# Where the last quarter's sum is made: in SBUF by GpSimd, or in HBM by a DMA that adds

## The chip, the core and the metric

The kernel runs on one core of one Trainium2 chip. The metric is the device time of that core in microseconds (us). The engines are TensorE (PE: matmuls; PEld: its weight loads), VectorE (DVE), ScalarE (ACT), GpSimd (POOL) and SyncE (SP). SP issues most DMA transfers, on a queue of its own; POOL can issue some too, on another. All data and sums are 32-bit floats.

## The reference

The input x has 4096 rows (32 x 128 tokens) of 2048 features. A weight is quantized to levels of a codebook with a low-rank correction, x is multiplied by it, and the result goes through a linear layer with a routed low-rank mixture; x is added at the end:

```python
def _L0_cond_ref(x, weight, scale_log, codebook, lora_A, lora_B):
    lora_delta = lora_B @ lora_A * (LORA_ALPHA / LORA_RANK)
    ...
    idx = jnp.searchsorted(thresholds, normalized, side='left')
    quantized = cb[idx]
    ...
    w_eff = w_q + lora_delta
    return x @ w_eff.T

def _L0_ffn_ref(x, W_base, b_base, A_w, B_w, router_w, cores):
    result = jnp.einsum('bsd,od->bso', x, W_base) + b_base
    ax = jnp.einsum('bsd,rd->bsr', x, A_w)
    probs = jax.nn.softmax(jnp.einsum('bsd,ed->bse', x, router_w), axis=-1)
    per_expert = jnp.einsum('bsr,erq->bseq', ax, cores)
    mixed = jnp.einsum('bseq,bse->bsq', per_expert, probs)
    return result + jnp.einsum('bsr,or->bso', mixed, B_w) * SCALING

x = x + _L0_ffn_ref(_L0_cond_ref(x, ...), ...)
```

## The kernel before

The two large linear maps and the added x are first folded into one 2048 x 2048 matrix S (quantized weight times base weight, plus the identity). This first stage ends at about 1000 us of the profile. It writes S to HBM (`s_dram`) already in the form that the second stage wants: 49 combinations of its sixteenths, 1024 KB each.

The second stage computes the output, transposed, as S times x, by the Strassen-Winograd scheme on two levels: seven products instead of eight for 2 x 2 blocks, and each of the seven again by seven. The tokens are cut into 4 groups (`NG`) of 1024 (`TG`); each group takes 7 outer x 7 inner = 49 products (`NP`), so there are 196, numbered n. A product (`product`, L833) is 32 matmuls (L846) of a tile of S with a block of 256 columns of x or of a difference of such blocks (`t`, made by `inner`, L813). The outer products come in the order `OUTER = [1, 5, 6, 2, 3, 7, 4]`; within a group, outer product 1 is n = 0 to 6, 5 is 7 to 13, 6 is 14 to 20, 2 is 21 to 27, 3 is 28 to 34, 7 is 35 to 41, and 4 is 42 to 48.

Each group keeps four tiles of half the features by half the tokens in SBUF, 2 MB each, in pools with one buffer. They turn into the four quarters of the group's output:

- `M1` is outer product 1; with outer product 2 added it is the upper left quarter.
- `M5` is outer product 5.
- `U2` is outer product 6 plus M1. With outer product 7 added (n = 35 to 41) it is a sum, U3. From n = 45 on outer product 4 is subtracted from it in place, block by block, and it becomes the lower left quarter.
- `C12` is U2 + M5, taken at n = 22 before U2 gets outer product 7; with outer product 3 added it is the upper right quarter.
- The lower right quarter is U3 + M5. `join` (L957) makes it at n = 43 on GpSimd, in M5's place, as it makes C12 at n = 22: four sums of 128 x 1024 elements (L964).

A sum that writes a block of U2 after n = 43 must wait until whatever reads the old block is done: L912 (DVE) for the upper left block after n = 45; L937, L916 and L941 (POOL) after n = 46 for the lower ones.

The work around the products is written out by hand. `early`, `late` and `last` hold what is to be issued at each n of a group, and the loop at L1083 runs through all n: the `early` entries, the product, the `late` entries, the next `inner`, the load of S for product n + 3 (`load_s`, L797), and the sums that take product n - 1 out of PSUM (`after`, L918). Every engine and queue executes its own part of this in order. S has three buffers (`stp`), so the load for product n + 3 waits on SP until product n is done. At n = 43 `early` also loads four times 1024 KB of x for the next group (`load_x`, L790, `xA` and `xB`); at n = 15 two for xB. The stores are issued on SP too: `store_half` (L1029) stores half of a quarter's features, 1024 KB in rows of 2 KB.

PSUM is four tiles of two banks each (`ps_z`), taken in turn by the products.

Of the kernel before, what the change touches and what calls it, by code (L numbers as in the profile page):

```python
# [16 lines left out]
ALU = mybir.AluOpType  # L17
# [150 lines left out]
def adaln_ffn_kernel(  # L168
# [29 lines left out]
    nc = tc.nc  # L198
# [16 lines left out]
    HT = TG // 2  # L215
# [15 lines left out]
    NK = NS // 4  # L231
    HB = NK * 2
# [41 lines left out]
    with ExitStack() as sa:  # L274
# [371 lines left out]
        at = {}  # L646
# [63 lines left out]
        for i in range(4, NS):  # L710
            g, j = divmod(i, 4)
# [74 lines left out]
    outr = outT.rearrange("(c p) t -> p c t", p=P)  # L786
    state = {}
# [15 lines left out]
    def blk(x, a, b):  # L803
        return x[:, a * NK : (a + 1) * NK, b * QT : (b + 1) * QT]
# [83 lines left out]
    def new(t, g):  # L888
        state[t, g] = home[t].tile([P, HB, HT], F32, tag=t, name=f"{t}_{g}")
        return state[t, g]  # L890
# [63 lines left out]
                lambda d: nc.vector.tensor_tensor(d, state["u3", o], z["e"], ALU.subtract),  # L954
            )

    def join(t, g, parts):  # L957

        u = state["U2", g]
        m5 = state["M5", g]  # L960
        out = new("C12", g) if t == "C12" else m5
        for a in range(2):
            for b in range(2):
                nc.gpsimd.tensor_tensor(blk(out, a, b), blk(u, a, b), blk(m5, a, b), ALU.add)  # L964
# [64 lines left out]
    def store_half(t, g, ph, th, a):  # L1029
        c = HB * ph + NK * a  # L1030
        nc.sync.dma_start(outr[:, c : c + NK, ts(2 * g + th, HT)], state[t, g][:, ts(a, NK)])

    def store_last(t, g, ph, th):

        c = HB * ph + NK
        for h in range(2):
            to = outr[:, c + 2 * h : c + 2 * h + 2, (2 * g + th) * HT : (2 * g + th) * HT + QT]
            nc.sync.dma_start(to, blk(state[t, g], 1, 0)[:, 2 * h : 2 * h + 2])
# [3 lines left out]
    early, late, last = {}, {}, {}  # L1042

    def at(where, n, f, *args):
        where.setdefault(n, []).append((f, args))
# [12 lines left out]
    at(late, 12, softmax)  # L1058
    at(late, 15, flip)
    at(late, 17, mix)  # L1060
    at(late, 22, lambda g: join("C12", g, None))
    at(late, 43, lambda g: join("C22", g, None))
    for t, n, ph, th in (("M1", 29, 0, 0), ("C12", 36, 0, 1), ("M5", 44, 1, 1)):
        for a in range(2):
            at(late, n + 2 * a, lambda g, *a: store_half(a[0], g, *a[1:]), t, ph, th, a)
    at(late, 47, lambda g: store("U2", g, 1, 0, 0, 0))
    at(late, 49, lambda g: (store("U2", g, 1, 0, 0, 1), store("U2", g, 1, 0, 1, 1)))
    at(last, 49, lambda g: store_last("U2", g, 1, 0))


# [83 lines left out]
```

## Time and profile before

| | us |
|---|---|
| median of 3 runs (2416.7 to 2417.75) | 2417.7 |
| the profiled execution, its time | 2421.27 |
| its span, from the first to the last instruction | 2419.5 |
| mean granted TensorE clock | 0.990 |
| POOL: the four sums of `join` into C12, mean of one (L964, x16) | 2.841 |
| POOL: the four sums of `join` into M5, mean of one (L964, x16) | 2.349 |
| POOL: a DMA issue of 512 KB, mean (L585, x10) | 0.719 |

The span is cut by the profile into busy time by engine, groups of instructions by source line, waits, and the chain of work that ended last. A group line has the source line, engine, operation, output and inputs by name, their shape and the count; then busy time and mean duration, then idle time before it and what ended it. A timeline line has the start, the duration (of several merged instructions together with the gaps between them), engine, line, operation and count. A DMA line has the issuing queue, size, and the median time from issue to landing.

The page's account of the DMA queues (packets, MB, share of 16 engines over the span) and of HBM:

```profile
q1 hardware_dynamic: 143248, 547.39, 63.5%
q0 software_dynamic: 2560, 9.18, 1.0%
HBM read 455.07 MB, written 101.71 MB: 230 GB/s over the span
```

q1 is SP's queue. q0 is POOL's; before, only the last part of the first stage uses it.

### The profile page before, as it was taken

Reading aid. Unit: us, or ns where it says so; the run is one execution under the profiler, and the core shown is the slowest. Engines: PE = TensorE matmul, PEld = TensorE weight load, DVE = VectorE, ACT = ScalarE, POOL = GpSimd, SP = SyncE. Lnnn points to the kernel's source line nnn. Section 1 sums busy time; section 2 is a strip of 40 time slices with the busy share of each in tenths; the row PEclk is TensorE's granted clock in tenths of the full one; section 3 lists DMA queues with packets and bytes.
Section 4 is the critical chain, followed back from the end, with each engine's and each line's share of the span. In section 5 each row is a group of like instructions: output and inputs, shape, how many; then the busy total and the mean of one; then the engine's idle time right before and its main releaser. Section 6 shows DMA issues by size and latency. Waiting matters only on the chain.

```text
span 2419.5 us, 23942 instructions
## 1 busy us (share of the span) xinstructions
PE 2332.1 (96%) x10032; PEld 1633.4 (68%) x10032; DVE 925.1 (38%) x788; ACT 370.9 (15%) x411; POOL 1045.2 (43%) x520
## 2 busy tenths in 40 slices
PE   3779999999999999999999999999999999999999
PEld 2334444444444444688888888888888888888887
DVE  7633348446745730433321223222333222323321
ACT  3623332343234300000000000000000000000000
POOL 5747888667766731571413103313203114003133
PEclk9989999999999999999999999999999999999999
DMA  5569998756966695594366754466645557563654
GB/s 169 224 250 330 373 357 315 277 211 228 339 225 227 242 345 188 182 341 182 140 235 231 240 198 174 174 211 256 228 176 185 195 193 263 206 223 142 209 188 160
DMA packets 146393, 558.47 MB, mean 231 GB/s; under 512 B 14360, under 2 KB 24864, under 8 KB 105312
## 3 DMA queue, kind: packets, MB, share of 16 engines
q1 hardware_dynamic: 143248, 547.39, 63.5%
q0 software_dynamic: 2560, 9.18, 1.0%
q8 instruction: 79, 1.29, 0.2%
q10 hardware_dynamic: 464, 0.26, 0.0%
q14 instruction: 42, 0.34, 0.0%
HBM read 455.07 MB, written 101.71 MB: 230 GB/s over the span
## 4 chain that ended last, share of the span: by engine, by line
PE 89%; DMA 4%; POOL 1%; SPq 0%; ACT 0%; DVE 0%; issue 0%; DVEq 0%; POOLq 0%
PE z L846 56%; PE m L514 24%; PE m L490 4%; PE z L876 1%; PE acc L612 1%; DMA t_dram<-tt 1%; PE d L352 1%; DMA xs<-in_xT 1%; DMA tt<-in_wbT 1%; DMA wbp_raw<-in_wbT 1%; PE m_r L592 1%; PE mx_ps L1013 0%; POOL tt L641 0%; POOL tt L640 0%; POOL tt L639 0%; PE ra L970 0%
## 5 line engine op out<-in xcount | busy, mean ns | idle before, releaser
L846 PE MATMUL z<-t,s 128*128 128x256 f32 x3584 | 791.3, 380 | 0.0
L846 PEld LDWEIGHTS z<-t,s 128*128 128x128 f32 x3584 | 677.7, 190 | 102.8 <-issue 12.5
L370 DVE COPY_PREDICATED a<-above,step 128x1024 f32<-128x1024 uint8 x192 | 251.1, 1308 | 159.9 <-ACT above L369 144.1
L490 PE MATMUL m<-wbp_raw,a 128*128 128x512 f32 x512 | 239.5, 625 | 31.1 <-DVE a L395 29.3
L846 PE MATMUL z<-xA,s 128*128 128x256 f32 x1152 | 254.5, 379 | 0.0
L514 PE MATMUL m<-wbp_raw,a 128*128 128x512 f32 x576 | 253.1, 596 | 0.0
L514 PE MATMUL m<-wbp,a 128*128 128x512 f32 x576 | 251.6, 595 | 0.0
L937 POOL TENSOR_TENSOR c<-u,m 128x1024 f32<-128x1024 f32 x16 | 49.8, 3111 | 444.4 <-DVE u L934 423.0
L846 PEld LDWEIGHTS z<-xA,s 128*128 128x128 f32 x1152 | 218.9, 190 | 30.2 <-issue 0.5
L369 ACT ACTIVATE above<-w,neg_t 128x1024 fp8e5<-128x1024 f32 x192 | 205.3, 1139 | 130.9 <-POOL w L361 114.8
L490 PEld LDWEIGHTS m<-wbp_raw,a 128*128 128x128 f32 x512 | 100.2, 200 | 157.0 <-issue 122.9
L514 PEld LDWEIGHTS m<-wbp,a 128*128 128x128 f32 x576 | 108.1, 190 | 135.1 <-issue 130.3
L514 PEld LDWEIGHTS m<-wbp_raw,a 128*128 128x128 f32 x576 | 107.6, 190 | 135.7 <-issue 128.8
L846 PE MATMUL z<-xB,s 128*128 128x256 f32 x768 | 169.8, 379 | 0.0
L846 PE MATMUL z<-xC,s 128*128 128x256 f32 x768 | 169.7, 379 | 0.0
L846 PEld LDWEIGHTS z<-xB,s 128*128 128x128 f32 x768 | 145.8, 190 | 20.2 <-ACT m L932 0.4
L846 PEld LDWEIGHTS z<-xC,s 128*128 128x128 f32 x768 | 145.9, 190 | 19.8
L937 POOL TENSOR_TENSOR M<-u,m 128x1024 f32<-128x1024 f32 x8 | 24.8, 3104 | 303.5 <-DVE u L934 303.5
L926 ACT COPY m<-z 128x1024 f32<-128x1024 f32 x28 | 28.4, 1013 | 811.1 <-PE z L846 811.1
L389 POOL TENSOR_TENSOR a<-a,w 128x1024 f32<-128x1024 f32 x30 | 76.5, 2550 | 119.7 <-DVEq L380 99.4
L928 DVE TENSOR_TENSOR u<-z,m 128x1024 f32<-128x1024 f32 x28 | 34.2, 1223 | 217.8 <-issue 174.3
L395 DVE TENSOR_TENSOR a<-a,ds 128x1024 f32<-128x1024 f32 x32 | 85.2, 2662 | 81.6 <-POOL a L391 80.8
(216 smaller groups left out, 1997.2 us busy)
## 6 DMA issues: line engine op xcount, KB each, us to landing
s<-s_dram SPq DMA_DIRECT2D x196, 1024.0 KB, 4.9
wbp_raw<-in_wbT SPq DMA_DIRECT2D x76, 1024.0 KB, 6.7
wbp<-t_dram SPq DMA_DIRECT2D x48, 1024.0 KB, 6.3
xs<-in_xT SPq DMA_DIRECT2D x64, 512.0 KB, 8.1
xA<-in_xT SPq DMA_DIRECT2D x24, 1024.0 KB, 9.4
s_dram<-z SPq DMA_DIRECT2D x46, 512.0 KB, 4.6
w<-in_weight SPq DMA_DIRECT2D x32, 512.0 KB, 6.3
tt<-in_wbT SPq DMA_DIRECT2D x32, 512.0 KB, 9.0
```

What stands on the lines that cost most here:

```text
L352: nc.tensor.matmul(d[:, 4 * h + n, :], lora_BT_sb[rows, f, n, :], st[i]["la"][rows], start=True, stop=True)
L369: nc.scalar.activation(above, q, AF.Relu, bias=neg_t[:, r : r + 1], scale=GAIN, saturate=False)
L370: nc.vector.copy_predicated(a, above.bitcast(U8), step[:, r : r + 1].to_broadcast([P, F // 2]))
L389: v.tensor_tensor(a, a, w, ALU.subtract)
L395: nc.vector.tensor_tensor(a, a, st[i]["ds", f], ALU.add)
L490: nc.tensor.matmul(z, a[:, s, CM * c + m, :], t[:, m, :], start=f == 0 and c == 0 and m == 0, stop=f == 1 and c == 1 and m == CM - 1,)
L514: nc.tensor.matmul(z, a[:, s, CM * c + k, :], pieces[key][:, k, :], start=c == 0 and k == 0, stop=c == 1 and k == CM - 1,)
L592: nc.tensor.matmul(ps[RP * j : RP * j + RP, 0], ra_sb[:, m, :], a_half(i, m // HM)[:, m % HM, :], start=m < 4, stop=m >= NM - 4, tile_posi ...
L846: nc.tensor.matmul(z[:, c, :], s[:, k, ts(c, P)], rhs[:, k, :], start=not more and k == 0 and c % PER == 0, stop=k == NK - 1 and c % PER = ...
L926: nc.scalar.copy(temp("m1", o), z["a"])
L928: nc.vector.tensor_tensor(temp("u2", o), z["b"], state["m1", o], ALU.add)
L937: lambda d: nc.gpsimd.tensor_tensor(d, state["u3", o], state["m5", o], ALU.add),
```

## The change

The lower right quarter is no longer summed in SBUF. M5 is stored to its place in the output as soon as it is complete, at n = 16 and 18, and at n = 43 two DMAs issued by GpSimd add U2 (which then holds U3) onto it in HBM, half of the features each. `join` at n = 22 is unchanged.

```diff
-    def join(t, g, parts):
+    def join(g):
 
         u = state["U2", g]
         m5 = state["M5", g]
-        out = new("C12", g) if t == "C12" else m5
+        out = new("C12", g)
         for a in range(2):
             for b in range(2):
                 nc.gpsimd.tensor_tensor(blk(out, a, b), blk(u, a, b), blk(m5, a, b), ALU.add)
...
+    def store_more(t, g, ph, th, a):
+        c = HB * ph + NK * a
+        nc.gpsimd.dma_start(
+            outr[:, c : c + NK, ts(2 * g + th, HT)], state[t, g][:, ts(a, NK)], accum_op=ALU.add
+        )
+
...
-    at(late, 22, lambda g: join("C12", g, None))
-    at(late, 43, lambda g: join("C22", g, None))
-    for t, n, ph, th in (("M1", 29, 0, 0), ("C12", 36, 0, 1), ("M5", 44, 1, 1)):
+    at(late, 22, join)
+    for a in range(2):
+        at(late, 43, lambda g, a: store_more("U2", g, 1, 1, a), a)
+    for t, n, ph, th in (("M5", 16, 1, 1), ("M1", 29, 0, 0), ("C12", 36, 0, 1)):
         for a in range(2):
             at(late, n + 2 * a, lambda g, *a: store_half(a[0], g, *a[1:]), t, ph, th, a)
```

## The prediction

> **What bounds the kernel now.** I read the page first, then the chain of waits, then the time windows, the timeline and the DMA issues around the place that is changed. The page's busy row, its chain and two windows of the first group, at the place where GpSimd now sums (the columns of a window: stretch, its length, busy time of PE, PEld, DVE, ACT and POOL with counts, clock, DMA share, GB/s):
>
> ```profile
> PE 2332.1 (96%) x10032; PEld 1633.4 (68%) x10032; DVE 925.1 (38%) x788; ACT 370.9 (15%) x411; POOL 1045.2 (43%) x520
> PE 89%; DMA 4%; POOL 1%; SPq 0%; ACT 0%; DVE 0%; issue 0%; DVEq 0%; POOLq 0%
> 1311.60:1318.80 7.20, 7.20 (x35) 6.33 (x34) 0.67 (x1) 0.58 (x1) 6.51 (x3) 1.00 0.91 334
> 1318.80:1326.00 7.20, 7.20 (x35) 6.35 (x34) 0.56 (x1) 0.96 (x1) 0.00 (x0) 1.00 1.05 387
> ```
>
> TensorE sets the time. From 1001.7 us on it runs the 4 groups of 49 products with no gap worth the name: a group takes 353.15 us (the chain's pieces at 1348.01, 1701.15 and 2054.30), some 7.2 us a product. In the two windows PE is full and the clock is 1.00, while POOL works or idles as it likes. But the last two columns say that the DMA engines are also full here, at 334 to 387 GB/s. So at this place TensorE and the DMA engines have no room left, and GpSimd has plenty.
>
> The timeline of the same place (start, duration, engine, line), and issues with their time to landing; the last three lines are narrow stretches around one issue each, the S load for product 46 of groups 0, 1 and 2:
>
> ```profile
> 1305.62 3.26 POOL L916 TENSOR_TENSOR U<-U,c 128x1024 f32<-128x1024 f32 x1 [3.80 <-DVE c L954]
> 1308.84 9.27 POOL L964 TENSOR_TENSOR M<-U,M 128x1024 f32<-128x1024 f32 x4
> 1341.44 3.20 POOL L937 TENSOR_TENSOR c<-u,m 128x1024 f32<-128x1024 f32 x1 [23.33 <-DVE u L934]
> 1332.86 7.17 PE L846 MATMUL z<-t,s 128*128 128x256 f32 x32
> 1311.16 0.32 SPq L800 DMA_DIRECT2D s<-s_dram  x1
> 1311.53 0.98 SPq L794 DMA_DIRECT2D xA<-in_xT  x2
> 1312.55 2.93 SPq L794 DMA_DIRECT2D xB<-in_xT  x2
> 1318.07 0.34 SPq L800 DMA_DIRECT2D s<-s_dram  x1
> 1318.45 0.43 SPq L1031 DMA_DIRECT2D outT<-M  x1
> ...
> s<-s_dram SPq DMA_DIRECT2D x1, 1024.0 KB, 11.2
> s<-s_dram SPq DMA_DIRECT2D x1, 1024.0 KB, 13.2
> s<-s_dram SPq DMA_DIRECT2D x1, 1024.0 KB, 11.3
> ```
>
> SP issues S of product 45 at 1311.16, four loads of x for the next group (4 x 1024 KB), and at 1318.07 S of product 46, which sits behind them; product 46 begins at 1332.86. The load lands 11.2 us after its issue, at 1329.3: 3.6 us to spare. In group 1 it is issued at 1671.2, lands 13.2 us later at 1684.4, and is wanted at 1686.0 (353.14 us after group 0): 1.6 us. In group 2: 2024.35 + 11.3 = 2035.65, wanted at 2039.15: 3.5 us. Of all 196 S loads the median lands in 4.9 us; this one is the tight one. The first half of the M5 store, issued at 1318.45, stands behind it in the same queue.
>
> **The change, part by part.**
>
> *Removed: four GpSimd sums a group*, 9.27 us on the POOL row above. Worth nothing: after them POOL idles 23.33 us until L937. Without that cover they would delay L937, and by it the U2 stores. M5's buffer comes free earlier too, but its next writer is the next group's second outer product (n = 56 on), ten products after the last of its stores now.
>
> *Moved: the two M5 stores, from n = 44 and 46 to 16 and 18, on SP's queue.* They wait for nothing there: M5's last block is written at 1103.02 (DVE, L954), and SP comes to n = 16 at about 1113.8. At n = 15 SP loads 2 x 1024 KB of xB; the windows of group 0 there (7.2 us each) show a DMA share of 1.01 from 1109.8 to 1117.0 and 0.50 in the next. The store's first half adds 1.05 MB; at 0.395 MB/us (the saturated windows' 387 to 410 GB/s) that is 2.7 us, just what the half-empty window holds. It is issued behind the S load of product 18, so the next one (19) could be the late one; that has about 10 us of room (14.8 us from issue to use, 4.9 to land). The second half meets a window with share 0.12 or 0.45. Cost 0; if all of it collided, 2.7 us of those 10.
>
> *Added: two DMA issues on POOL at n = 43*, each 1024 KB. The trace has POOL issues of plain stores: 572 ns for 256 KB (L583), 720 ns for 512 KB (L585), so by a straight line 1.0 us for 1024 KB, and perhaps twice that if each row also needs its read described. POOL reaches the place at 1308.84, as the sum does now, so both are out by about 1311 to 1313. The price lies in the 23.33 us of idleness: 0. Their wait for the M5 stores, made at n = 18, has long been over at n = 43. Behind them on POOL stands nothing before L937.
>
> *Added: the transfers.* No row of this trace shows a DMA that adds. Call f its engine time as a multiple of a plain transfer of the same 1.05 MB. Low end: the row of the M5 store, which it resembles on the outside, f = 1. Above: it must fetch the destination from HBM as the xA load does (1024 KB, 9.4 us to land) and read SBUF and write HBM as the M5 store does (1024 KB, 11.9 us): one of each, f = 2. Far end: nothing overlaps, and each packet pays the round trip of the smallest load, 1.8 us (8 KB of cores). POOL's queue moves 9.18 MB in 2560 packets, 3.6 KB each, so a half has 18 per engine: 33 us, f = 33/2.66 = 12. I take f = 2, because the load and the store are the two rows that it is made of, and the S, x and POOL rows of this trace overlap their round trips well enough to reach 390 GB/s.
>
> Do they share engines with SP's loads? An S load issued at 1036.2 us beside 1.84 MB of POOL stores landed in 8.2 us instead of 4.8, in windows with a share of 1.02 to 1.04. So yes.
>
> Sum: up to the landing of S 46 the engines must now do 2.1 f MB more. Two credits: the stretch from 1309 to 1312 moves 0 GB/s now, and gives the POOL queue about 1.25 us alone (0.5 MB); and of the M5 store some 0.55 MB went through beside S 46 (6.84 MB moved from 1312 to 1330, of which S 45, x and S 46 are 6.29), which is gone. Delay = (2.1 f - 1.05) / 0.395: f = 1: 2.7 us; f = 2: 8.0; f = 3: 13.3; f = 4: 18.6. Less the room of 3.6, 1.6 and 3.5 us in groups 0, 1, 2: at f = 2 PE stops for 4.4 + 6.4 + 4.5 = 15.3 us; at f = 1, 1.1 us; at f = 3, 31.2; at f = 4, 47.1. Group 3 loads no further x (its windows show share 0.42 there), so 0. Nothing wins this back: PE is full before and after. S 47 is 2.7 us behind S 46 in the queue and wanted 7 us behind it: no second stall. DVE's L912 (1333.03, waits for the first half to be read) and POOL's L916 at 1344.71 (second half) come after the loads that are late, so they add nothing until f is near 4.
>
> The tail: PE ends at 2414.56, the span at 2419.5, with the same last U2 stores: 0. The sum against the profiled execution: span 2419.5 + 15.3 = 2434.8. That run took 2421.27, 3.6 above the median of 2417.7; on the median, 2433.0.
>
> The Trainium skill has a rule that speaks against the change. "Collectives: The Full Stack", on the bandwidth ceiling, says that an add in a DMA is slowed not by the arithmetic but by its two source reads, with a measured ratio of 62.28 to 32.35, or 1.93. No row here shows such a transfer; by that figure the stalls would be 4.0 + 6.0 + 4.1 = 14.1 us, beside 15.3 by the rows.
>
> **The rivals.** *No visible stall:* one pass, or SP's queue served ahead of POOL's. For it: 1 MB stores from SBUF do run beside loads at 390 GB/s. Against: the destination has to be read somewhere. It decides below f = 1.35, where the stalls sum to 4.8 us. At f = 1: 2417.7 + 1.1 = 2418.8. This is the case on the other side.
>
> *The transfers land too late:* f of 4 and more, up to 12, with the engines idle between round trips, so that SP's loads slip through but the transfers end late. At the far end the second half lands 66 us after issue, near 1375, and L916 at 1344.71 is 30 us late; SP's store of that block (n = 49, issued at 1355.56 now) holds SP until some 1377, with S loads behind it that have 10 us of room: 11 us a group, 33 in three. In the last group 2368.3 + 66 = 2434, then three POOL operations of 2.35 and a store of 7.7 us: 2449, 29 past the present end. In all 62: 2480. For it: each row waits for its own read. Against: the same is true of any copy.
>
> *Faster through a freer GpSimd or buffer:* nothing on PE's rows waits for the sums. The only part that PE does not fill is the 4.9 us of the tail; even half of it would be 2.4 us: 2415.3.
>
> **How the numbers follow.** 0.2% is 4.8 us, about what a measurement of this kernel can tell from no change. Forecast (f from 1.35 to 4; 2423 to 2465, 2433.0 the likeliest): 0.62. Late landing: 0.10. No visible stall: 0.25. Faster: 0.03. So slower 0.72, same 0.25, faster 0.03. The range goes from 2417, f = 1 with nothing lost, to 2466, f = 4.
>
> **What would show it.** Right: PE's weight load of product 46 waiting for S in groups 0 to 2 and not in 3, S 46 landing some 19 to 21 us after issue, POOL's queue larger by 8.4 MB (4 groups of 2.1) or twice that if both reads are counted, HBM reads up by 8.4 MB, gaps of 4 to 6 us. S 46 landing in less than 14 us would show that f is smaller than I take it, or that SP's queue is favoured. Wrong: gaps at another product, such as 19 (M5 stores) or 52 (SP held by a U2 store), or POOL's issues taking over 20 us.

## The result, and the profile after

The changed kernel takes 2444.3 us (median of 4 runs, 2442.9 to 2445.5) beside 2417.3 before (also 4 runs, one more than in the table above): 27.0 us slower, a ratio of 1.0112 (95% interval 1.0094 to 1.0129). The forecast was 2433.0, in a range of 2417 to 2466: the sign and the place are as forecast, the loss is 1.8 times the 15.3 us of the sum.

The page after (busy time; queue POOL: packets, MB, share; HBM; a group of PE):

```profile
PE 2334.9 (96%) x10032; PEld 1637.9 (67%) x10032; DVE 923.7 (38%) x788; ACT 370.8 (15%) x411; POOL 1018.5 (42%) x512
...
q0 software_dynamic: 6784, 17.57, 3.0%
...
HBM read 455.07 MB, written 110.10 MB: 231 GB/s over the span
...
L846 PE MATMUL z<-t,s 128*128 128x256 f32 x3584 | 798.5, 382 | 20.4 <-DMA s<-s_dram 20.4
```

The last line reads, before:

```profile
L846 PE MATMUL z<-t,s 128*128 128x256 f32 x3584 | 791.3, 380 | 0.0
```

POOL lost its sums, and with the new issues it is busy 27 us less in all; PE did not wait for any of that. PE's busy time has hardly changed, but a group of its matmuls that never stood idle now does, for 20.4 us, on the loads of S. The waits of PE in the second stage name the same 20.4 us in three places (total, times, longest):

```profile
PE z L846 <- DMA s<-s_dram: 20.4, 3, 7.0
```

Where it happens, in the timeline of the first group:

```profile
1304.57 2.64 POOL L1035 DMA_DIRECT2D outT<-U  x2
1306.90 0.32 SPq L800 DMA_DIRECT2D s<-s_dram  x1
1307.28 2.78 SPq L794 DMA_DIRECT2D xA<-in_xT  x2
1310.10 10.12 SPq L794 DMA_DIRECT2D xB<-in_xT  x2
1320.33 25.50 SPq L800 DMA_DIRECT2D s<-s_dram  x4
1327.52 1.15 PE L876 MATMUL z<-mx,bw_sb 17*128 17x256 f32 x16
1335.51 9.97 PE L846 MATMUL z<-t,s 128*128 128x256 f32 x32 [6.84 <-DMA s<-s_dram]
```

The adding transfers go out at 1304.57, the four x loads just behind them. Before, the second pair of x loads was issued within 2.93 us; now SP is held for 10.12 us while it issues them. So S of product 46, the first of the four in the line, is issued only at 1320.33 and lands 15.1 us later, at 1335.4:

```profile
s<-s_dram SPq DMA_DIRECT2D x1, 1024.0 KB, 15.1
```

Product 46 could have begun at about 1328.7 and begins at 1335.51. Groups 1 and 2 show the same (waits of 6.55 and 6.97 us), group 3, which loads no further x, nothing.

One more thing is in the last line of the timeline: the product that follows the wait takes 9.97 us, not 7.17. The windows around it show the clock (the last three columns are the granted clock, DMA share and GB/s):

```profile
1327.50:1328.70 1.20, 1.17 (x17) 0.72 (x16) 0.00 (x0) 0.00 (x0) 0.00 (x0) 1.00 1.06 389
1328.70:1335.50 6.80, 0.00 (x0) 0.00 (x0) 2.36 (x2) 0.00 (x0) 0.00 (x0) 0.67 1.04 413
1335.50:1338.50 3.00, 2.99 (x7) 2.45 (x8) 0.00 (x0) 0.00 (x0) 0.00 (x0) 0.50 0.94 391
1338.50:1341.50 3.00, 3.00 (x9) 2.35 (x9) 0.00 (x0) 0.00 (x0) 0.00 (x0) 0.55 0.03 11
1341.50:1345.40 3.90, 3.90 (x20) 3.44 (x19) 0.00 (x0) 0.00 (x0) 0.00 (x0) 1.00 0.00 0
```

During the wait the granted clock falls, and the product runs at half of it until about 1341.2, its first 5.7 us: 7 matmul records in 3 us where a full clock gives some 15. In the three groups product 46 takes 9.97, 9.60 and 9.21 us, together 7.3 more than three times 7.17. Waits and slow products make 20.4 + 7.3 = 27.7 us. The time from one group to the next went from 353.15 to 362.2 us, 27.2 in three groups. So the whole loss is accounted for.

### The profile page after: what moved, and what is told of

Read it like the earlier page. It is cut to its first block, busy times and chain, and to the rows that moved or that the text cites. A ratio compares the mean times of both kernels' runs of the same rounds, so it can differ in the third digit from the quotient of the medians.

```text
span 2443.0 us, 23948 instructions
## 1 busy us (share of the span) xinstructions
PE 2334.9 (96%) x10032; PEld 1637.9 (67%) x10032; DVE 923.7 (38%) x788; ACT 370.8 (15%) x411; POOL 1018.5 (42%) x512
## 3 DMA queue, kind: packets, MB, share of 16 engines
HBM read 455.07 MB, written 110.10 MB: 231 GB/s over the span
## 4 chain that ended last, share of the span: by engine, by line
PE 71%; DMA 2%; POOL 2%; SPq 1%; issue 0%; ACT 0%; DVE 0%; DVEq 0%; POOLq 0%
PE z L846 55%; PE m L514 14%; DMA s<-s_dram 2%; PE z L876 1%; SPq L794 1%; DMA xs<-in_xT 0%; PE acc L612 0%; PE d L352 0%; PE mx_ps L1013 0%; POOL a L389 0%; POOL a L390 0%; POOL z L580 0%; POOL z L578 0%; POOL a L391 0%; PE m_r L592 0%
## 5 line engine op out<-in xcount | busy, mean ns | idle before, releaser
L846 PE MATMUL z<-t,s 128*128 128x256 f32 x3584 | 798.5, 382 | 20.4 <-DMA s<-s_dram 20.4
L846 PEld LDWEIGHTS z<-t,s 128*128 128x128 f32 x3584 | 682.9, 191 | 125.5 <-DMA s<-s_dram 21.6
L490 PE MATMUL m<-wbp_raw,a 128*128 128x512 f32 x512 | 234.6, 614 | 30.3 <-DVE a L395 30.2
L846 PE MATMUL z<-xA,s 128*128 128x256 f32 x1152 | 254.5, 379 | 0.0
L514 PE MATMUL m<-wbp_raw,a 128*128 128x512 f32 x576 | 253.1, 596 | 0.0
L846 PEld LDWEIGHTS z<-xA,s 128*128 128x128 f32 x1152 | 218.9, 190 | 30.2 <-issue 0.5
L846 PE MATMUL z<-xB,s 128*128 128x256 f32 x768 | 169.7, 379 | 0.0
L846 PE MATMUL z<-xC,s 128*128 128x256 f32 x768 | 169.7, 379 | 0.0
L846 PEld LDWEIGHTS z<-xB,s 128*128 128x128 f32 x768 | 145.9, 190 | 19.8
L846 PEld LDWEIGHTS z<-xC,s 128*128 128x128 f32 x768 | 145.9, 190 | 19.8
```

What stands on the lines that cost most here:

```text
L490: nc.tensor.matmul(z, a[:, s, CM * c + m, :], t[:, m, :], start=f == 0 and c == 0 and m == 0, stop=f == 1 and c == 1 and m == CM - 1,)
L514: nc.tensor.matmul(z, a[:, s, CM * c + k, :], pieces[key][:, k, :], start=c == 0 and k == 0, stop=c == 1 and k == CM - 1,)
L846: nc.tensor.matmul(z[:, c, :], s[:, k, ts(c, P)], rhs[:, k, :], start=not more and k == 0 and c % PER == 0, stop=k == NK - 1 and c % PER = ...
```

## The experiments

The theory, "engine time": an adding transfer holds the DMA engines about twice as long per MB as a plain one, and together with the x loads that stand ahead of S 46 on SP's queue this pushes that load past its use. The first rival is "adding is special": it is the read of the destination, and not the time on the engines, that blocks others. The second is "place": any 2 MB on GpSimd's queue at this moment would do the same. A third asks what the slow product 46 comes from. Each ratio is to the kernel before, measured beside that run, with its 95% interval.

### The same transfers without the addition, once and twice

```diff
-            outr[:, c : c + NK, ts(2 * g + th, HT)], state[t, g][:, ts(a, NK)], accum_op=ALU.add
+            outr[:, c : c + NK, ts(2 * g + th, HT)], state[t, g][:, ts(a, NK)]
```

> The two transfers at n = 43 stay on GpSimd's queue but store U2 plainly over the M5 that was stored before, so the lower right quarter is U2 and not the sum. Theory 'engine time' (the adding transfers hold the DMA engines about 2.3 times as long per MB as plain ones, and push the S load of product 46 past its use): with f = 1 that load is 2.7 us later than before, against room of 3.6, 1.6 and 3.5 us: 2417 to 2420. Theory 'place' (any 2 MB on GpSimd's queue at this moment holds up SP's issue of the x loads and so the S load behind them, whatever it does): near 2444, at least 2435.

Measured: 2420.1 us, ratio 1.0011 (1.0001 to 1.0020). For the second run a copy to a scratch tensor is added:

```diff
+        nc.gpsimd.dma_start(copy_dram[g][:, ts(a, NK)], state[t, g][:, ts(a, NK)])
```

> As the run with one plain store, but each half is stored twice from GpSimd, once to the output and once to a scratch tensor in HBM: 4.2 MB of plain transfers, f = 2, no adding; the lower right quarter is again U2 alone. Theory 'engine time': the S load of product 46 is 8 us late, PE waits 4.4 + 6.4 + 4.5 = 15 us, and the product after each wait runs some 2 us slower at the lower clock: 2433 to 2441. Theory 'adding is special' (the read of the destination before its write holds up other transfers beyond its bytes): twice the plain bytes does much less than the adding, under 2427.

Measured: 2443.6 us, ratio 1.0107 (1.0090 to 1.0124), just above the range expected and as slow as the changed kernel. The waits of PE with one plain store, then with two (its L847 is L846 of the others, a line further down):

```profile
PE z L846 <- DMA s<-s_dram: 2.0, 2, 1.0
```

```profile
PE z L847 <- DMA s<-s_dram: 18.4, 3, 6.5
```

And product 46 of the first group with two:

```profile
1336.06 9.96 PE L847 MATMUL z<-t,s 128*128 128x256 f32 x32 [6.50 <-DMA s<-s_dram]
```

Two plain transfers do what one adding transfer does, down to the wait and the slow product: waits of 18.4 us and products 46 of 9.96, 9.93 and 9.85 us (8.2 more than three times 7.17) make 26.6 us, all of its loss. The first two rivals fall: the addition needs no effect beyond the time that it takes on the engines to explain the loss, and one plain transfer at this place costs some 3 us (with an interval that hardly excludes 0). How long each holds the engines can be read from POOL's queue, in the DMA answer for 1304 to 1336 us (packets, MB, share of 16 engines); first the changed kernel with SP's queue above it, then one plain store, then two:

```profile
q1 hardware_dynamic: 2570, 7.47, 60.9%
q0 software_dynamic: 1056, 2.10, 38.0%
```

```profile
q0 software_dynamic: 544, 2.10, 19.0%
```

```profile
q0 software_dynamic: 832, 4.19, 35.3%
```

38.0% of 32 us is 12.2 us of all engines for 2.10 MB, 19.0% is 6.1: f = 2.0. With two plain stores it is 35.3% for 4.19 MB, or 5.65 us per 2.10 MB, f = 2.15.

### One part of the change alone

The early stores of M5 added to the kernel before:

```diff
+    for a in range(2):
+        at(late, 16 + 2 * a, lambda g, a: store_half("M5", g, 1, 1, a), a)
```

> The kernel before, with the two early stores of M5 at n = 16 and 18 added; the sum on GpSimd and the stores of it at n = 44 and 46 stay, so the quarter is stored twice. Both theories on the stall at product 46: the early stores cost nothing, 2416 to 2420. If they delay the S load of product 19 or 20, or hold SP, it shows here: above 2422, with a PE wait near n = 19.

Measured: 2417.2 us, ratio 1.0005 (0.9995 to 1.0014); PE waits for no load of S. And the adding transfers without those stores:

```diff
-    for t, n, ph, th in (("M5", 16, 1, 1), ("M1", 29, 0, 0), ("C12", 36, 0, 1)):
+    for t, n, ph, th in (("M1", 29, 0, 0), ("C12", 36, 0, 1)):
```

> The changed kernel without the early stores of M5: the lower right quarter lacks M5, the adding transfers add U2 to what the output holds from the start. The adding transfers alone cause the loss: 2442 to 2447, with the same wait at product 46. If the early stores had a share, it is smaller by that share.

Measured: 2443.1 us, ratio 1.0110 (1.0093 to 1.0127), and the waits of PE:

```profile
PE z L846 <- DMA s<-s_dram: 19.8, 3, 6.9
```

The adding transfers alone make the loss.

### The x loads moved away

```diff
-    at(early, 43, lambda g: g + 1 < NG and (load_x("xA", g + 1, 0, 0), load_x("xB", g + 1, 0, 1)))
+    at(early, 44, lambda g: g + 1 < NG and load_x("xA", g + 1, 0, 0))
+    at(early, 46, lambda g: g + 1 < NG and load_x("xB", g + 1, 0, 1))
```

> The changed kernel with the loads of x for the next group moved: xA from n = 43 to 44, xB from 43 to 46. Theory 'engine time': up to the S load of product 46 the engines then move 2.1 MB of S and the adding transfers (2.1 x 2.3 = 4.8 MB worth), 6.9 MB or 17.5 us, so it lands near 1328 of the old time scale and is wanted at 1332.9; S 47 has xA before it, 10 MB or 25.4 us, wanted 7 us later: no wait, 2416 to 2420. If the adding transfers delay PE by something other than the queue ahead of S 46 (their landing late, DVE or POOL waiting for them), the time stays above 2430.

Measured: 2417.5 us, ratio 1.0002 (0.9992 to 1.0012). The whole loss is gone, with the adding transfers in place. The same move in the kernel before:

> The kernel before with the loads of x moved as in the run that had the changed kernel back at 2417.5 (xA to n = 44, xB to 46). If that move is worth nothing by itself, since PE has no wait to lose in the kernel before: 2416 to 2419. If the move brought a gain that hid a loss of the changed kernel, this is faster than 2414.

Measured: 2417.3 us, ratio 1.0001 (0.9991 to 1.0010): the move is worth nothing there. The changed kernel's timeline with it:

```profile
1306.85 2.65 POOL L1035 DMA_DIRECT2D outT<-U  x2
...
1316.47 1.05 SPq L794 DMA_DIRECT2D xA<-in_xT  x2
...
1330.30 0.98 SPq L794 DMA_DIRECT2D xB<-in_xT  x2
1330.89 7.17 PE L846 MATMUL z<-t,s 128*128 128x256 f32 x32
```

SP is no longer held (1.05 and 0.98 us for two issues), and product 46 starts without a wait at 1330.89.

### The same bytes at the same time, on another queue

Moving the loads spreads the work and also takes it from in front of S 46. To part the two, ScalarE issues the x loads in place of SP (`load_x` gets the queue as an argument):

```diff
+    at(early, 43, lambda g: g + 1 < NG and [load_x(t, g + 1, 0, h, nc.scalar) for t, h in (("xA", 0), ("xB", 1))])
```

> The changed kernel with the four loads of x at n = 43 issued by ScalarE, on its own queue, at the same point and of the same bytes. The DMA engines have the same work up to the end of the burst; only what stands ahead of the S load of product 46 in its queue is gone. If that place in SP's queue is what turns busy engines into a wait: S 46 is issued when product 43 is done and shares the engines with two other queues, 1.05 MB at a third of 0.37 MB/us or 8.5 us, before its use 14.8 us after issue: no wait, 2416 to 2421. If the amount of work alone decides: 2435 to 2445. ScalarE is held while it issues (SP was held 13 us), but its next copy out of PSUM has 13 us of room.

Measured: 2417.5 us, ratio 1.0004 (0.9994 to 1.0014). But the trace has ScalarE issue them at 1290.08 to 1292.4 us, well ahead of the adding transfers at 1302.8, since nothing held it; so this run moved the loads in time and does not answer the question. With `at(last, 43, ...)` they stand behind ScalarE's copy of product 42:

> The first run with the x loads on ScalarE's queue let them go 14 us earlier (1290 instead of 1307 us), since nothing held ScalarE there, so it moved them as well as changing their queue. Here they stand behind ScalarE's copy of product 42 out of PSUM, and so go out at about 1308, as on SP: the same bytes at the same time, and only the place ahead of the S load of product 46 is gone. If that place in SP's queue turns busy engines into a wait: S 46 is issued when product 43 is done, shares the engines with two other queues, lands in some 9 us and is in time: 2416 to 2421. If the amount of work at that moment decides, whatever the queue: 2435 to 2446.

Measured: 2416.7 us, ratio 0.9999 (0.9989 to 1.0008). The timeline, and then two windows:

```profile
1306.65 2.65 POOL L1035 DMA_DIRECT2D outT<-U  x2
...
1309.16 2.08 ACTq L794 DMA_DIRECT2D xA<-in_xT  x2
1311.41 2.89 ACTq L794 DMA_DIRECT2D xB<-in_xT  x2
...
1330.69 7.17 PE L846 MATMUL z<-t,s 128*128 128x256 f32 x32
```

```profile
1315.00:1318.00 3.00, 3.00 (x16) 2.64 (x15) 1.22 (x1) 0.00 (x0) 0.00 (x0) 1.00 1.05 338
1324.00:1327.00 3.00, 3.00 (x16) 2.64 (x15) 0.00 (x0) 0.00 (x0) 0.00 (x0) 1.00 1.07 290
```

Its DMA issues, S 46 and one of the xB loads:

```profile
s<-s_dram SPq DMA_DIRECT2D x1, 1024.0 KB, 9.6
...
xB<-in_xT ACTq DMA_DIRECT2D x1, 1024.0 KB, 31.7
```

The xA and xB loads leave 2.5 and 4.8 us after the adding transfers begin to be issued (2.7 and 5.5 in the changed kernel), the engines are full (share 1.05 and 1.07), and yet nothing is lost: S 46 lands in 9.6 us, and the xB load, which nobody needs yet, takes 31.7. The kernel before has the same 4.2 MB ahead of S 46 and loses nothing, and this run has the same added work and loses nothing. It takes both: the added work, and an urgent load that stands behind 4.2 MB that are not urgent, on one queue.

The Trainium skill, "DMA: Bandwidth & Descriptors", section "Issuing engines are not separate DMA queues", says that starting transfers on several engines saves only the sequencer's time to issue them. For the bytes per second these runs agree: 429 GB/s from 1330 to 1333 us before, with SP's queue alone, and 419 from 1333 to 1336 us in this run, with SP's and ScalarE's. For the time of one urgent load they do not: another queue for the x loads was worth 27 us here, and the measurement decides. Part of that is the sequencer's time, as the section has it, since SP's issue of S 46 was 6.5 us late; but S 46 also landed 9.6 us after its issue, not 15.1. No run parts the two.

### The wait filled with work

To see whether the product after the wait is slow because PE stood still, matmuls with the identity are put before the mixture that follows product 45, into the PSUM tile that the mixture overwrites:

```diff
+        if n % NP == 45 and g + 1 < NG:
+            for k in range(32):
+                nc.tensor.matmul(
+                    state["z", o, KEY[7]][:, k % 4, :], ident, blk(live["xC"], 1, 0)[:, k % 4, :],
+                    start=True, stop=True, skip_group_check=True,
+                )
```

> The changed kernel, and in groups 0 to 2, before the mixture that follows product 45, 32 further matmuls of the same size with the identity as weights, into the PSUM tile that the mixture then overwrites. They take 6.9 us, about what PE waits there (6.84, 6.55, 6.97). Theory 'clock after a wait' (the product after the wait takes 9.2 to 10.0 us in place of 7.2 because PE stood still before it): the wait is filled, the product takes 7.2 again, and the time falls by 6 to 7 us, to 2437 to 2439. If that product is slow for another reason (the full DMA engines, its operands), the time stays at 2444 or rises by up to 1 us.

Measured: 2458.6 us, ratio 1.0171 (1.0154 to 1.0188): slower, not faster. The size was wrong: each `nc.tensor.matmul` of the code is two PE instructions (a product has 16, the profile's 32), so 32 of them take 13.8 us. Taken for what it is, the run still speaks: 3 x 13.8 = 41.4 us on top of 2417.0 make 2458.4, so the waits and the slow products are both gone; its trace shows no wait of PE for S. With 16 (L871 in the timeline; L882 is the mixture):

> As the run with added matmuls, with half of them: there each call turned out to be two PE instructions, so the 32 calls took 13.8 us in each of three groups, more than the wait they were to fill. 16 calls take 6.9 us. Theory 'clock after a wait': PE then waits at most 1 to 4 us more where the load is later than that, the product that follows takes 7.2 to 7.5 us, and the time falls from 2444 to 2437 to 2440. If that product is slow for another reason, 2444 to 2446.

Measured: 2439.1 us, ratio 1.0096 (1.0079 to 1.0113), within what was expected. The first group:

```profile
1328.74 7.07 PE L871 MATMUL z<-xC,ident 128*128 128x256 f32 x32
1335.74 1.15 PE L882 MATMUL z<-mx,bw_sb 17*128 17x256 f32 x16
1337.05 7.17 PE L846 MATMUL z<-t,s 128*128 128x256 f32 x32 [0.17 <-DMA s<-s_dram]
```

Here the load is as late as before, useless work fills the time, and product 46 takes 7.17 us in all three groups. The loss is 22.6 us instead of 27.0, each against the kernel before beside it; the intervals of the two ratios overlap, so the trace shows this better than the times do. So the slow product is a consequence of the standstill. "TensorE: Matmul & The Clock Gate", Part 1, states a rule for this: after an idle window of about 3.4 us the clock falls to half, and it takes some 3.4 us of work to come back. The traces agree in kind: the clock is 0.50 after the waits of 5.9 to 7.0 us, and with one plain store a wait of 0.96 us left the next product at 7.17 us. The times vary. In groups 0 to 2 of the changed kernel the clock fell 2.3, 4.7 and 4.3 us after PE's last matmul and was full again 5.7, 4.9 and 4.2 us after the next one began. In all it was low for 10.2, 6.8 and 6.8 us, near three and two times the page's figure.

## Why the prediction was right, and where its size was off

*What bounds the kernel, and where the change would bite.* Right: TensorE without gaps, DMA engines full where the next group's x is loaded, S 46 the load with the least room. PE waits for S at product 46 of groups 0 to 2 and nowhere else.

*The removed sums, the moved stores, the issues on POOL: 0 each.* Right. The early stores alone measure 1.0005 (0.9995 to 1.0014). POOL's issues took 1.28 to 1.82 us against 1.0 to 2, inside its idle time.

*f = 2.* Right: 2.0 and 2.15 by the shares of the queue, and two plain transfers in its place give the same time. The far end (12) and the low end (1) are both out. The expectations of the first experiments took f = 2.3, which I had worked out from the waits; the shares say that the missing delay was elsewhere. The ratio of 1.93 that the prediction quotes beside it, from transfers between ranks, lies near both readings.

*The sum.* This is the step that failed, in two terms. The delay of S 46 was put at (2.1 f - 1.05) / 0.395 = 8.0 us in every group. From the issue of S 45 to the landing of S 46 it took 18.1 us before (1311.16 to 1329.3) and 28.5 after (1306.90 to 1335.4): 10.4 us more, and in the same way 8.2 and 10.5 in groups 1 and 2.

The first term is the credits. That of 0.55 MB, for the M5 store that no longer runs beside S 46, did not exist. S 45, x and S 46 are 6.29 MB; in those stretches SP's queue moved 6.56, 7.28 and 6.61 MB before and 7.14, 7.07 and 7.18 after. So 0.8 to 0.9 MB of loads behind S 46 went through beside it after the change, more than the 0.3 MB before in groups 0 and 2, and less than the 1.0 MB in group 1, where the delay is smallest. The other credit, 1.25 us for POOL's queue alone, was half of that: from 1304.57 to 1306.90 the queue took 27.1% of the engines, 0.63 us. Without the first credit the delay is 9.4 us and the waits 5.8 + 7.8 + 5.9 = 19.5 us, beside 6.84 + 6.55 + 6.97 = 20.4 measured. The sum fits better than the groups do. That the credits are the cause is worked out from these figures; no run tried it alone.

The second term was missing: PE's clock after the wait, 7.3 us. "Nothing wins this back" was true, but something added to it. With both: 19.5 + 7.3 = 26.8, measured 27.0; that it is so close is in part luck, since group 1 is 1.2 us too long in it and the others 1.0 and 1.1 too short. It is luck too that the measured time lies well inside the range: the range was drawn for other values of f, and by the prediction's formula 27.0 us would need f = 2.7, where the shares show 2.

*The rivals.* No visible stall: it nearly happens with f = 1 (2418.8 forecast for it, 2420.1 measured, with waits of 2.0 us where 1.1 were worked out), and it happens with f = 2 when another queue carries the x loads. Landing too late: the adding transfers landed in a median of 13.4 us, at most 18.7, and DVE's L912 waited for PE alone. Faster by a freer GpSimd: no sign of it.

*Signs that I named.* S 46 landing 19 to 21 us after its issue was not seen (15.1, 13.8, 15.0), because SP's issue itself was held up by 6.5 us; counted from the end of product 43 it is some 22. The 13.8 would by itself have been read as a smaller f; the shares show 2. The gaps of PE are 6.55 to 6.97 us, not 4 to 6. HBM reads were to rise by 8.4 MB: the counter stayed at 455.07, and only the written bytes rose, by 8.39. So the counter leaves the read of the destination out.

No run was measurably faster than the kernel before: PE is full there, and there is nothing in it for this change to free.

## What to carry to other kernels

A transfer is priced by the engine time that it takes and by the load that it makes late: look for the load with the least room between landing and use, and see whether the new work comes before it. The DMA that adds took the engines twice as long here as a plain one of the same bytes; put it where the engines are half empty, or keep the urgent loads on a queue without bulk in front of them. When a wait of several us lands on TensorE, add to it the slow matmuls that follow.

## What the runs showed of the hardware that was not expected

- An adding transfer in rows of 2 KB goes in packets of 2 KB: POOL's queue has 4224 packets more than before for 8.39 MB, against 2176 more (4736 in all) for the same bytes stored plainly. The GB/s column counts its bytes once, so it reads 126 to 205 GB/s from 1306 to 1312 us while the engines are full (share 0.91 and 1.13).
- Issuing a load can hold the issuing engine: the two xB issues held SP for 10.12 us after the change, 2.93 before, and 5.25 with one plain store. With the x loads behind ScalarE's copy of product 42 they held ScalarE for 17.24 us in group 1, and its next copy began at 1681.72; PE did not wait for it.
- After a wait of 6 to 7 us PE ran at a clock of 0.50 for 4.2 to 5.7 us more. From its fall to its return the clock was low for 10.2, 6.8 and 6.8 us in the three groups, and for the same times with two plain stores; the product after the wait lost 2.0 to 2.8 us. A wait of 0.96 us left no trace in the next product.
